# Layer 0 of a four-layer graph network: s products of two blocks issued together, the fifth slot group summed for four blocks, slot groups 172 columns apart

## The chip, the cores and the metric

One core of a Trainium2 chip runs the whole kernel in one launch. The metric is device time in microseconds (us). Five engines work side by side, each through its own queue in order: TensorE (PE, with its weight loads listed apart as PEld), VectorE (DVE), ScalarE (ACT), GpSimd (POOL) and SyncE (SP, which issues most DMAs). They wait for one another through semaphores.

## The reference, cut to what matters

A feature matrix x of 2708 rows by 128 columns goes through four layers with a sparse adjacency matrix adj of 2708 by 2708 (about 2.3% of its entries are not zero). Only layer 0 is touched by the change:

```python
s = node_feats @ msg_w[:, :D].T
d = node_feats @ msg_w[:, D:].T
messages = jax.nn.gelu(s[:, None, :] + d[None, :, :] + msg_b, approximate=False)
aggregated = jnp.einsum('ijd,ij->id', messages, adj)
combined = jnp.concatenate([node_feats, aggregated], axis=-1)
new_feats = combined @ upd_w.T + upd_b
h = jax.nn.gelu(new_feats, approximate=False) + node_feats
```

So for every edge (i, j) a gelu of s[i] + d[j] is needed, weighted by adj[i, j] and summed over j into row i. Layers 1 to 3 (gated attention, a hyperbolic layer, two propagation steps) follow.

## The kernel before

**Tiles and blocks.** Layer 0 takes the rows in 22 row tiles (LT) of 125 rows (LR), each as five groups (NC) of 25 rows (RG). The columns j are cut into 22 blocks (NB) of 124 (JB). In a block, each row has five slots (CAP); a slot holds one of the row's edges in the block. 25 rows times five slots fill 125 of 128 partitions, so a block's five groups of rows give five slot groups, each a set of columns of one PSUM tile `sl`: 128 columns for s + d and 25 columns for the edge weights (DA = 153). Edges beyond the five slots of a block go a second way: the largest 16 per row are searched out on DVE (`largest`, `where`), their d rows are fetched by indirect DMAs on POOL (`fetch`), and they are added by `far_gelu` (ACT) and `far_sum` (DVE).

**One block**, loop at L1021. `pick` (L944) multiplies one-hot selectors S (124 by 128, fp16, made on DVE by `slot`) with dA, the table of d and of the adjacency weights, in a high and a low fp16 part: ten products of 153 columns, one pair per slot group, into `sl`. Then two s products add s to the 128 columns of each group: `same` (50 rows, one-hot) times `s3`; s3 keeps groups 0 to 2 on partitions 0 to 49 and groups 3 and 4 on partitions 64 to 113, so one product uses the upper and one the lower half of the rows of the PE array. ACT takes a gelu of the block's message columns (L1028) into g; `weigh` (L1014) lets DVE multiply the 25 weight columns of each slot with `own`, which gives W. `add_up` (L957) sums over slots: per slot group, W (128 by 32) times g (128 by 128), fp32, into one PSUM bank `acc`. Its output is 32 partitions, so four groups use four column strips of the array side by side. It is called for a pair of blocks; groups 0 to 3 of both go to column 0 of acc, the fifth groups of both to column 1, on partitions 0 to 31 and 32 to 63.

**PSUM.** Three `sl` tiles of two banks each are used in turn (L1025), one bank is shared by `rank`, `rank_row` and `turn` (p_misc), one holds acc.

**Order.** Within `tc.manual_schedule()` each engine runs what is issued, in the order of the Python code. Everything around the block loop is a list of steps with a block number to be issued at (`Rows.when`, L748): loads of adjacency blocks (SP), masks and ranks (`find`, `rank`, `rank_row`: DVE, PE, ACT), selectors (`slot`), spilled edges (`past`, `largest_of`, `where`), for the following row tiles. In each pass of the loop the order is: steps due earlier, pick, gelu, weigh of the block before, steps due at this block; `late` collects blocks whose slot sums are outstanding, and LAG = 3 sends the sums of the oldest two after the steps of every even block. A row tile's sums end in `agg` (L971), which `turn` (L930) brings into transposed form, with `spread` and `fold` adding the 32-row strips.

Lines that the text names: L820 `rank`'s product, L821 its copy on ACT, L828 and L833 the high and low part of the adjacency weights (ACT, DVE), L840 selectors, L861 `rank_row`'s products, L872 `past`, L879 the block maxima, L910 the search, L914 the indirect fetch, L920 and L928 gelu and sums of the far edges, L950 picks, L955 s products, L966 slot sums, L1015 W, L1028 gelu.

Of the kernel before, what the change touches and what calls it, by code (L numbers as in the profile page):

```python
# [14 lines left out]
F32 = mybir.dt.float32  # L15
# [3 lines left out]
ALU = mybir.AluOpType  # L19
# [3 lines left out]
P = 128  # L23
# [149 lines left out]
def gnn_stack(ctx: ExitStack, tc: tile.TileContext, t, out: bass.AP):  # L173
# [378 lines left out]
    with ExitStack() as l0:  # L552
# [10 lines left out]
        with ExitStack() as msg:  # L563
# [4 lines left out]
            sq_tab = dram.tile([2, NT * P, D], FP16, name="sq_tab")  # L568


            DA = D + RG
            dA = [mp.tile([JB, NB, NC, DA], FP16, name=f"dA{q}") for q in range(2)]


# [53 lines left out]
            ep = msg.enter_context(tc.tile_pool(name="slots", bufs=5))  # L628
# [24 lines left out]
            class Piece:  # L653
# [7 lines left out]
                def products(self):  # L661
                    b0, b1, a0, a1 = self.b0, self.b1, self.a0, self.a1
                    psd, pss = (sl_all[(2 * self.n + k) % 3][:, 0, :].rearrange("p (b d) -> p b d", d=D)
                                for k in range(2))
                    d = self.d = ep.tile([P, 6, D], F32, name="g")[:JB, :b1 - b0, :]
                    room = gp.tile([P, 8, D], F32, name="far")
                    s = self.s = room[:, :a1 - a0, :]
                    parts = room[:, 4:, :].rearrange("p i d -> p (i d)").bitcast(FP16)
                    self.parts = parts.rearrange("p (q i d) -> p q i d", q=2, d=D)[:, :, :a1 - a0, :]
                    if N < b1 * JB:  # L670
                        nc.vector.memset(d, 0.0)
                    if N < a1 * P:
                        nc.vector.memset(s, 0.0)
                    for b in range(b0, b1):
                        r = min(JB, N - b * JB)
                        nc.tensor.matmul(psd[:r, b - b0, :], xT[:, b * JB:b * JB + r], msg_d, start=True, stop=True)
                    for i in range(a0, a1):
                        nc.tensor.matmul(pss[:rows[i], i - a0, :], xT[:, i * P:i * P + rows[i]], msg_s,
                                         start=True, stop=True)
                    full = min(b1, NFB) - b0  # L680
                    nc.scalar.copy(d[:, :full, :], psd[:JB, :full, :])
                    if full < b1 - b0:
                        r = N - NFB * JB
                        nc.scalar.copy(d[:r, full, :], psd[:r, full, :])
                    self.hi, self.lo = (v[:, b0:b1, :, :D] for v in dA)
                    nc.scalar.activation(self.hi[:, :, 0, :], d, AF.Copy, scale=D_SCALE)
                    self.spread(self.hi)
                    for a, b, r in groups():
                        if a0 <= a < a1:
# [12 lines left out]

                def update(self):
                    ps = p_out.tile([P, PB, D], F32, name="acc")
                    u = ep.tile([P, 6, D], F32, name="g")[:, :self.a1 - self.a0, :]
# [32 lines left out]
            class Rows:  # L738
# [191 lines left out]
                def turn(self):  # L930
# [3 lines left out]
                    nc.tensor.matmul(ps[:, :32 * NC], self.extra, spread.rearrange("p c i -> p (c i)"),  # L934
                                     start=True, stop=False)
                    nc.tensor.matmul(ps[:, :P], a[:, 0, :], ident, start=False, stop=False)
                    nc.tensor.matmul(ps[:, P:32 * NC], a[:HALF, 1, :], fold, start=False, stop=True)

                def close(self):
                    nc.scalar.copy(aggT[:, self.r0:self.r0 + LR].rearrange("p (c i) -> p c i", c=NC),  # L940
                                   self.ps_t[:, :32 * NC].rearrange("p (c i) -> p c i", c=NC)[:, :, :RG])


                def pick(self, b, sl):  # L944

                    h, n = divmod(b, HB)
                    group = [sl[:, c // 3, c % 3 * DA:(c % 3 + 1) * DA] for c in range(NC)]
                    for c in range(NC):
                        for q in range(2):
                            nc.tensor.matmul(group[c], self.S[h][:, n, c, :], dA[q][:, b, c, :],  # L950
                                             start=c % 3 == 0 and q == 0, stop=False)
                    for k, (a, e) in enumerate(spans(0, NC, 3)):
                        p = slice(k * HALF, k * HALF + 2 * RG)
                        out = sl[:, k, :(e - a) * DA].rearrange("p (c e) -> p c e", c=e - a)[:, :, :D]
                        nc.tensor.matmul(out, same[p], self.s3[p, :e - a, :], start=False, stop=True)  # L955

                def add_up(self, pair):  # L957


                    if pair[0][0] == 0:  # L960
                        self.acc = p_out.tile([P, PB, D], F32, name="acc")[:, :2, :]
                    jobs = [(b, g, W, c, c * 32, 0) for b, g, _, W in pair for c in range(4)]
                    jobs += [(b, g, W, 4, b % 2 * 32, 1) for b, g, _, W in pair]
                    for b, g, W, c, q, k in jobs:
                        ends = b == NB - 1 and q >= HALF or b >= NB - 2 and k == 1
                        nc.tensor.matmul(self.acc[q:q + 32, k, :], W[:, c, :], g[:, c, :],  # L966
                                         start=b == 0 and k == 0, stop=ends)
                    if pair[-1][0] == NB - 1:
                        self.agg = up.tile([P, 2, D], F32, name="agg")
                        for k, m in ((0, P), (1, HALF)):  # L970
                            nc.scalar.activation(self.agg[:m, k, :], self.acc[:m, k, :], AF.Copy,  # L971
                                                 accum_out=tot[:m, self.t, k:k + 1])

            class Update:

# [8 lines left out]
                    nc.sync.dma_start(out=self.new, in_=u_tab.rearrange("(n p) d -> p n d", p=P))  # L984

                def open(self):
                    room = Values.within(ep.tile([P, 6, D], F32, name="g").rearrange("p a d -> p (a d)"))
                    V = Values.within(ep.tile([P, 6, D], F32, name="g").rearrange("p a d -> p (a d)"))
# [20 lines left out]
            assert NC == 5 and NB % 2 == 0  # L1009
            R = [Rows(i) for i in range(LT)]  # L1010
            steps = sorted(((g, n, step) for n, (g, step) in enumerate(x for v in [preparation(), *(v.when() for v in R), U.when()] for x in v)),
                           key=lambda x: x[:2])
            with tc.manual_schedule():
                def weigh(b, g, sl, W):  # L1014
                    nc.vector.tensor_tensor(  # L1015
                        W[:, :, :RG].rearrange("p (k c) i -> p k c i", k=2), columns_of(sl, D, DA),
                        own[:, None, None, :].to_broadcast([P, 2, 3, RG]), op=ALU.mult)


                late = []  # L1020
                for block in range(LT * NB):  # L1021
                    i, b = divmod(block, NB)
                    while steps and steps[0][0] < block:
                        steps.pop(0)[2]()
                    sl, W = sl_all[block % len(sl_all)], W_all[block % len(W_all)]  # L1025
                    R[i].pick(b, sl)
# [919 lines left out]
```

## Time and profile before

| what | value |
|---|---|
| median of three runs | 1902.93 us (1902.68 to 1903.74) |
| the profiled execution | 1905.26 us, of it the span 1903.5 us |
| mean granted TensorE clock | 0.918 |
| PE busy over the span | 1626.2 us (85%) |
| DVE busy over the span | 1436.1 us (75%) |
| ACT / POOL busy over the span | 1052.1 us (55%) / 630.8 us (33%) |
| first and last pick of layer 0 | 55.5 us and 879.7 us |
| picks L950: count, busy | 4840, 408.2 us |
| slot sums L966: records, busy | 4840, 205.5 us (each product is two records) |
| s products L955: count, busy | 968, 161.9 us |
| gelu L1028: count, mean | 484, 813 ns |
| W L1015: count, mean | 484, 300 ns |

Busy times of PE overlap, since matmuls are pipelined and their ends are modelled; starts are exact. A mean over the whole span mixes layers with different limits, so the stretch from 55 to 880 us is what has to be read for this change. A line's "idle before" is the time for which its engine had nothing running just before it, with the release that ended it.

### The profile page before, as it was taken

The numbers are of one execution on the slowest core, as the hardware profiler recorded it, in microseconds if no ns is written. First come the engines' busy times: TensorE is split into PE (matmuls) and PEld (weight loads), VectorE is DVE, ScalarE is ACT, GpSimd is POOL, SyncE is SP. The second block draws the span as 40 slices with busy tenths as digits, with TensorE's granted clock in tenths as the row PEclk, the third lists the DMA queues.
The fourth block names the chain that finished last, engine by engine and source line by source line (L and its number), as shares of the span: only waits on it lengthen the run. The fifth ranks groups of instructions, "written<-read, shape, count | busy, mean of one in ns | idle before, by whom it ended". The sixth has DMA issues, their size and how long they took to land.

```text
span 1903.5 us, 36624 instructions
## 1 busy us (share of the span) xinstructions
PE 1626.2 (85%) x14033; PEld 955.4 (50%) x14033; DVE 1436.1 (75%) x3607; ACT 1052.1 (55%) x1538; POOL 630.8 (33%) x426
## 2 busy tenths in 40 slices
PE   5899999999999999986599997577888897199995
PEld 5666666666666666655344443322223343044542
DVE  6899999999999999986678885838886783860104
ACT  3667667666766766654444444458886771430003
POOL 5667766776776677565100000000000000000000
PEclk8899999999999999998699998658998798599997
DMA  8666665666666576533134430032334463354431
GB/s 214 153 130 143 133 144 119 148 122 141 143 131 142 122 149 124 117 69 88 63 123 150 152 112 1 1 106 76 142 137 140 141 199 146 137 204 146 146 121 31
DMA packets 234896, 238.30 MB, mean 125 GB/s; under 512 B 28844, under 2 KB 219630, under 8 KB 228122
## 3 DMA queue, kind: packets, MB, share of 16 engines
q1 hardware_dynamic: 183670, 212.18, 36.1%
q0 software_dynamic: 51040, 23.68, 10.7%
q8 instruction: 112, 1.84, 0.4%
q14 instruction: 74, 0.61, 0.1%
HBM read 220.65 MB, written 15.15 MB: 124 GB/s over the span
## 4 chain that ended last, share of the span: by engine, by line
PE 43%; DVE 28%; POOL 8%; issue 7%; ACT 7%; DMA 5%; DVEq 0%; SPq 0%; ACTq 0%; POOLq 0%
PE acc L1843 10%; POOL far L914 8%; PE lg L1231 5%; PE acc L1238 5%; PE accV L1571 5%; DVE ix L910 5%; PE ps L1499 4%; DMA far<-d_tab,ix 3%; DVE W L1015 3%; PE sl L950 3%; DVE extra L928 2%; DVE o L872 2%; DVE S L840 2%; PE accO L1575 2%; DVE dA L833 1%
## 5 line engine op out<-in xcount | busy, mean ns | idle before, releaser
L914 POOL DMA_INDIRECT far<-d_tab,ix x352 | 563.0, 1600 | 257.5 <-DVE W L1015 110.6
L1028 ACT ACTIVATE g<-sl 128x768 f32<-128x768 f32 x484 | 393.3, 813 | 257.0 <-PE sl L955 201.0
L950 PE MATMUL sl<-dA,S 124*128 124x153 f16 x4840 | 408.2, 231 | 10.1 <-DVE W L1015 7.7
L950 PEld LDWEIGHTS <-S 124*128 124x128 f16 x4840 | 330.4, 98 | 79.7 <-issue 67.9
L966 PE MATMUL acc<-g,W 128*32 128x128 f32 x4840 | 205.5, 277 | 0.5 <-issue 0.5
L966 PEld LDWEIGHTS acc<-g,W 128*32 128x32 f32 x4840 | 140.6, 109 | 58.8 <-issue 55.5
L955 PE MATMUL sl<-s,same 50*128 50x384 f16 x968 | 161.9, 308 | 0.0
L1015 DVE TENSOR_TENSOR W<-sl,own 128x150 f32<-128x150 f32 x484 | 143.4, 300 | 14.6 <-ACT g L1028 13.4
L1232 ACT ACTIVATE w<-lg,row_L_gnn_gate_bias 128x512 f32<-128x512 f32 (+1 forms) x132 | 83.5, 636 | 108.2 <-PE lg L1231 106.9
L1486 POOL TENSOR_TENSOR arena<-arena,off 128x128 f32<-128x128 f32 (+1 forms) x22 | 21.6, 982 | 351.1 <-DMA arena<-in_adjT 321.3
L840 DVE TENSOR_SCALAR S<-rk 124x1000 f16<-124x1000 bf16 (+1 forms) x330 | 133.4, 430 | 0.0
L910 DVE FIND_INDEX8 ix<-v,o 128x8 uint32<-128x2728 f32 x44 | 131.7, 2993 | 0.0
L1571 PE MATMUL accV<-arena,X 128*128 128x512 f32 (+4 forms) x264 | 124.7, 592 | 6.5 <-DVE arena L1537 6.5
L1231 PE MATMUL lg<-qT,mT 128*128 128x512 f32 (+2 forms) x264 | 121.1, 547 | 3.6 <-ACT w L1232 3.1
L1238 PE MATMUL acc<-w,both 128*128 128x512 f32 (+2 forms) x264 | 121.2, 547 | 0.0
L928 DVE SCALAR_TENSOR_TENSOR extra<-far,v,extra 128x128 f32<-128x128 f32 x330 | 114.9, 348 | 6.3
L449 DVE TENSOR_TENSOR g<-ps,row_L_gnn_b 128x512 f32<-128x512 f32 (+2 forms) x14 | 7.9, 574 | 148.1 <-PE ps L447 148.0
L1499 PE MATMUL ps<-XT 128*128 128x512 f32 (+8 forms) x150 | 90.4, 691 | 32.2 <-ACT arena L1505 26.5
L872 DVE SCALAR_TENSOR_TENSOR o<-ps,ar 128x496 f32<-128x496 f32 x132 | 82.4, 624 | 37.0 <-issue 19.7
L1843 PE MATMUL acc<-at,x 128*128 128x512 f32 (+2 forms) x156 | 66.2, 574 | 48.4 <-ACT x L379 48.4
L1233 DVE TENSOR_TENSOR w<-w,at 128x512 f32<-128x512 f32 (+1 forms) x132 | 82.5, 625 | 27.1 <-ACT w L1232 27.1
L879 DVE MAX8 cand<-o 128x8 f32<-128x248 f32 x242 | 90.4, 411 | 0.0
(357 smaller groups left out, 2507.2 us busy)
## 6 DMA issues: line engine op xcount, KB each, us to landing
at<-in_adjT SPq DMA_DIRECT2D x42, 1354.0 KB
ar<-in_adj SPq DMA_DIRECT2D x105, 248.0 KB
far<-s_tab SPq DMA_DIRECT2D x44, 512.0 KB
at<-in_adjT SPq DMA_DIRECT2D x42, 448.0 KB
arena<-in_adjT SPq DMA_DIRECT2D x21, 704.0 KB
arena<-in_adjT SPq DMA_DIRECT2D x21, 650.0 KB
held<-in_adjT SPq DMA_DIRECT2D x7, 1354.0 KB
f_tab<-arena SPq DMA_DIRECT2D x10, 704.0 KB
```

The costliest lines, as they stand in the source:

```text
L840: nc.vector.tensor_scalar(self.S[h][:, :n, :, k * RG:(k + 1) * RG], self.rk[h][:, :n, :LR].rearrange("p b (c i) -> p b c i", c=NC), EDGE + ...
L910: nc.vector.max_index(ix, self.v[:, n * 8:n * 8 + 8], self.o.rearrange("p b j -> p (b j)"))
L914: nc.gpsimd.indirect_dma_start(out=self.far[n][:, k, :], out_offset=None, in_=d_tab[:, :], in_offset=bass.IndirectOffsetOnAxis(ap=self.ix[ ...
L950: nc.tensor.matmul(group[c], self.S[h][:, n, c, :], dA[q][:, b, c, :], start=c % 3 == 0 and q == 0, stop=False)
L966: nc.tensor.matmul(self.acc[q:q + 32, k, :], W[:, c, :], g[:, c, :], start=b == 0 and k == 0, stop=ends)
L1015: nc.vector.tensor_tensor(W[:, :, :RG].rearrange("p (k c) i -> p k c i", k=2), columns_of(sl, D, DA), own[:, None, None, :].to_broadcast([ ...
L1028: nc.scalar.activation(g.rearrange("p (k c) d -> p k c d", k=2), columns_of(sl, 0, D), AF.Gelu, scale=1.0 / D_SCALE)
L1231: nc.tensor.matmul(lg, mT[:, j * P:j * P + r], qT[:, a:b], start=True, stop=True)
L1238: nc.tensor.matmul(acc[k], mrow[:rows[j], j, :], ws[j][:rows[j], a:b], start=j == 0, stop=j == NT - 1)
L1499: nc.tensor.matmul(ps, XT[:, self.js], XT[:, c], start=True, stop=False)
L1571: nc.tensor.matmul(Pair.acc[0][:, a:b], X[:self.r, self.j, :], self.w_[:, a:b], start=first, stop=last)
L1843: nc.tensor.matmul(acc[k], src[:rows[j], j, :], at[:rows[j], a:b], start=j == order[0], stop=j == order[-1])
```

## The change

1. `begin` (new) issues the s products of two blocks, ahead of their picks, at every even block: for block b and b + 1, in their two `sl` tiles. They now start the accumulation (start=True) and cover all 153 columns of a group, since `s3` is kept with 25 zero columns per group (two tiles, zeroed once on POOL). The picks all add to that.
2. In the pair, the order becomes: s products of both blocks, picks of the first, its steps, picks of the second, its steps, and the slot sums of the pair before (LAG = 2, sent at odd blocks).
3. `add_up` keeps the fifth slot groups until four blocks have them (or the row tile ends, which it does with two), and puts them on four strips of 32 partitions. The second column of acc and of agg has 128 rows in place of 64, and `fold` adds four strips.
4. Slot groups start 172 columns apart over the two banks of an `sl` tile (0, 172, 344, 516, 688), so gelu and `weigh` handle five groups with one step, 640 and 125 elements per partition, where they handled six places, 768 and 150.
5. W has six tiles in place of five, and so has the pool of g.

```diff
-            DA = D + RG
+            DA, PITCH = D + RG, 172
...
-            fold = mp.tile([HALF, 32], F32, name="fold")
-            nc.vector.tensor_add(fold, ident[:HALF, :32], ident[:HALF, 32:HALF])
+            fold = mp.tile([P, 32], F32, name="fold")
+            nc.vector.tensor_add(fold, ident[:, :32], ident[:, 32:HALF])
+            for k in range(HALF, P, 32):
+                nc.vector.tensor_add(fold, fold, ident[:, k:k + 32])
...
-            W_all = [mp.tile([P, 6, 32], F32, name=f"W{n}") for n in range(5)]
+            W_all = [mp.tile([P, NC, 32], F32, name=f"W{n}") for n in range(6)]
+            s3_all = [mp.tile([P, 3, DA], FP16, name=f"s3{n}") for n in range(2)]
+            for v in s3_all:
+                nc.gpsimd.memset(v, 0.0)
...
-                return sl[:, :, :3 * DA].rearrange("p k (c e) -> p k c e", c=3)[:, :, :, a:b]
+                return sl.rearrange("p k n -> p (k n)")[:, :NC * PITCH].rearrange("p (c e) -> p c e", c=NC)[:, :, a:b]
...
-                    self.s3 = up.tile([P, 3, D], FP16, name="s3")
+                    self.s3 = s3_all[self.t % 2]
...
-                            nc.sync.dma_start(out=self.s3[p:p + RG, :e - a, :], in_=src[:, a:e, :])
+                            nc.sync.dma_start(out=self.s3[p:p + RG, :e - a, :D], in_=src[:, a:e, :])
...
-                    nc.tensor.matmul(ps[:, P:32 * NC], a[:HALF, 1, :], fold, start=False, stop=True)
+                    nc.tensor.matmul(ps[:, P:32 * NC], a[:, 1, :], fold, start=False, stop=True)
...
+                def begin(self, sl):
+
+                    for k, (a, e) in enumerate(spans(0, NC, 3)):
+                        p = slice(k * HALF, k * HALF + 2 * RG)
+                        nc.tensor.matmul(columns_of(sl, 0, DA)[:, a:e, :], same[p], self.s3[p, :e - a, :], start=True, stop=False)
+
                 def pick(self, b, sl):
 
                     h, n = divmod(b, HB)
-                    group = [sl[:, c // 3, c % 3 * DA:(c % 3 + 1) * DA] for c in range(NC)]
                     for c in range(NC):
                         for q in range(2):
-                            nc.tensor.matmul(group[c], self.S[h][:, n, c, :], dA[q][:, b, c, :],
-                                             start=c % 3 == 0 and q == 0, stop=False)
-                    for k, (a, e) in enumerate(spans(0, NC, 3)):
-                        p = slice(k * HALF, k * HALF + 2 * RG)
-                        out = sl[:, k, :(e - a) * DA].rearrange("p (c e) -> p c e", c=e - a)[:, :, :D]
-                        nc.tensor.matmul(out, same[p], self.s3[p, :e - a, :], start=False, stop=True)
+                            nc.tensor.matmul(columns_of(sl, 0, DA)[:, c, :], self.S[h][:, n, c, :], dA[q][:, b, c, :], start=False,
+                                             stop=q == 1 and c in (2, NC - 1))
...
-                    jobs += [(b, g, W, 4, b % 2 * 32, 1) for b, g, _, W in pair]
+                    self.fifth += [(b, g, W, 4, b % 4 * 32, 1) for b, g, _, W in pair]
+                    if len(self.fifth) == 4 or b1 == NB - 1:
+                        jobs += self.fifth
+                        self.fifth = []
...
-            LAG = 3
+            LAG = 2
...
+                    if b % 2 == 0:
+                        for k in range(2):
+                            R[i].begin(sl_all[(block + k) % len(sl_all)])
                     R[i].pick(b, sl)
-                    g = ep.tile([P, 6, D], F32, name="g")
-                    nc.scalar.activation(g.rearrange("p (k c) d -> p k c d", k=2), columns_of(sl, 0, D), AF.Gelu,
+                    g = ep.tile([P, NC, D], F32, name="g")
+                    nc.scalar.activation(g, columns_of(sl, 0, D), AF.Gelu,
                                          scale=1.0 / D_SCALE)
```

More of the change, by code (lines that the diff above doesn't have):

```diff
@@ L627, in gnn_stack @@
             up = msg.enter_context(tc.tile_pool(name="sums", bufs=2))
-            ep = msg.enter_context(tc.tile_pool(name="slots", bufs=5))
+            ep = msg.enter_context(tc.tile_pool(name="slots", bufs=6))
             p_misc = msg.enter_context(tc.tile_pool(name="ps_misc", bufs=1, space=PSUM))
@@ L664, in products @@
                                 for k in range(2))
-                    d = self.d = ep.tile([P, 6, D], F32, name="g")[:JB, :b1 - b0, :]
+                    d = self.d = ep.tile([P, NC, D], F32, name="g")[:JB, :b1 - b0, :]
                     room = gp.tile([P, 8, D], F32, name="far")
@@ L704, in update @@
                     ps = p_out.tile([P, PB, D], F32, name="acc")
-                    u = ep.tile([P, 6, D], F32, name="g")[:, :self.a1 - self.a0, :]
+                    u = ep.tile([P, NC, D], F32, name="g")[:, :self.a1 - self.a0, :]
                     if N < self.a1 * P:
@@ L941, in close @@
                                    self.ps_t[:, :32 * NC].rearrange("p (c i) -> p c i", c=NC)[:, :, :RG])
+                def begin(self, sl):
+                    for k, (a, e) in enumerate(spans(0, NC, 3)):
+                        p = slice(k * HALF, k * HALF + 2 * RG)
+                        nc.tensor.matmul(columns_of(sl, 0, DA)[:, a:e, :], same[p], self.s3[p, :e - a, :], start=True, stop=False)
                 def pick(self, b, sl):
                     h, n = divmod(b, HB)
-                    group = [sl[:, c // 3, c % 3 * DA:(c % 3 + 1) * DA] for c in range(NC)]
                     for c in range(NC):
                         for q in range(2):
-                            nc.tensor.matmul(group[c], self.S[h][:, n, c, :], dA[q][:, b, c, :],
-                                             start=c % 3 == 0 and q == 0, stop=False)
-                    for k, (a, e) in enumerate(spans(0, NC, 3)):
-                        p = slice(k * HALF, k * HALF + 2 * RG)
-                        out = sl[:, k, :(e - a) * DA].rearrange("p (c e) -> p c e", c=e - a)[:, :, :D]
-                        nc.tensor.matmul(out, same[p], self.s3[p, :e - a, :], start=False, stop=True)
+                            nc.tensor.matmul(columns_of(sl, 0, DA)[:, c, :], self.S[h][:, n, c, :], dA[q][:, b, c, :], start=False,
+                                             stop=q == 1 and c in (2, NC - 1))
                 def add_up(self, pair):
-                    if pair[0][0] == 0:
+                    b1 = pair[-1][0]
+                    if b1 == 1:
                         self.acc = p_out.tile([P, PB, D], F32, name="acc")[:, :2, :]
+                        self.fifth = []
                     jobs = [(b, g, W, c, c * 32, 0) for b, g, _, W in pair for c in range(4)]
-                    jobs += [(b, g, W, 4, b % 2 * 32, 1) for b, g, _, W in pair]
+                    self.fifth += [(b, g, W, 4, b % 4 * 32, 1) for b, g, _, W in pair]
+                    if len(self.fifth) == 4 or b1 == NB - 1:
+                        jobs += self.fifth
+                        self.fifth = []
                     for b, g, W, c, q, k in jobs:
@@ L967, in add_up @@
                                          start=b == 0 and k == 0, stop=ends)
-                    if pair[-1][0] == NB - 1:
+                    if b1 == NB - 1:
                         self.agg = up.tile([P, 2, D], F32, name="agg")
-                        for k, m in ((0, P), (1, HALF)):
-                            nc.scalar.activation(self.agg[:m, k, :], self.acc[:m, k, :], AF.Copy,
-                                                 accum_out=tot[:m, self.t, k:k + 1])
+                        for k in range(2):
+                            nc.scalar.activation(self.agg[:, k, :], self.acc[:, k, :], AF.Copy,
+                                                 accum_out=tot[:, self.t, k:k + 1])
             class Update:
@@ L986, in open @@
                 def open(self):
-                    room = Values.within(ep.tile([P, 6, D], F32, name="g").rearrange("p a d -> p (a d)"))
-                    V = Values.within(ep.tile([P, 6, D], F32, name="g").rearrange("p a d -> p (a d)"))
+                    room = Values.within(ep.tile([P, NC, D], F32, name="g").rearrange("p a d -> p (a d)"))
+                    V = Values.within(ep.tile([P, NC, D], F32, name="g").rearrange("p a d -> p (a d)"))
                     self.st = room.part([P, NT, 6])
@@ L1005, in rows @@
                     nc.gpsimd.tensor_tensor(x[:r, a:b, :], x[:r, a:b, :], over_tiles(ln_b, b - a, r), op=ALU.add)
-            LAG = 3
+            LAG = 2
             U = Update()
-            assert NC == 5 and NB % 2 == 0
+            assert NC == 5 and NB % 4 == 2
             R = [Rows(i) for i in range(LT)]
@@ L1015, in weigh @@
                     nc.vector.tensor_tensor(
-                        W[:, :, :RG].rearrange("p (k c) i -> p k c i", k=2), columns_of(sl, D, DA),
-                        own[:, None, None, :].to_broadcast([P, 2, 3, RG]), op=ALU.mult)
+                        W[:, :, :RG], columns_of(sl, D, DA), own[:, None, :].to_broadcast([P, NC, RG]),
+                        op=ALU.mult)
                 late = []
@@ L1025, in gnn_stack @@
                     sl, W = sl_all[block % len(sl_all)], W_all[block % len(W_all)]
+                    if b % 2 == 0:
+                        for k in range(2):
+                            R[i].begin(sl_all[(block + k) % len(sl_all)])
                     R[i].pick(b, sl)
-                    g = ep.tile([P, 6, D], F32, name="g")
-                    nc.scalar.activation(g.rearrange("p (k c) d -> p k c d", k=2), columns_of(sl, 0, D), AF.Gelu,
+                    g = ep.tile([P, NC, D], F32, name="g")
+                    nc.scalar.activation(g, columns_of(sl, 0, D), AF.Gelu,
                                          scale=1.0 / D_SCALE)
```

## The prediction

> **What bounds the kernel now.** Only layer 0 is edited, so I first read the busy time by stretch: layer 0's steady part, its last row tile but one, its last, and everything behind it (columns: length; busy time and instructions of PE, PEld, DVE, ACT, POOL; clock; DMA).
>
> ```profile
> 60.00:800.00 740.00, 705.80 (x10288) 507.02 (x10286) 696.67 (x1984) 504.75 (x752) 513.47 (x321) 1.00 0.65 134
> 800.00:845.00 45.00, 37.66 (x538) 26.58 (x536) 39.41 (x110) 26.65 (x39) 20.02 (x13) 1.00 0.39 86
> 845.00:885.00 40.00, 36.51 (x549) 27.25 (x547) 23.46 (x69) 22.28 (x35) 30.59 (x20) 1.00 0.48 87
> 885.00:1905.00 1020.00, 812.12 (x2468) 364.55 (x2466) 632.35 (x1357) 478.26 (x679) 36.62 (x35) 0.86 0.33 117
> ```
>
> Two engines are full at once: PE 95% and DVE 94% of the steady part, at full clock; ACT (68%) is not. The starts of the first pick in each row tile lie 37.03 us apart (20 of the 22 tiles are near that; tile 20 takes 43.7). So a PE saving is worth only what DVE can follow. The timeline of one pair of blocks gives PE's prices (start, length, engine, line; ends are modelled, so I use start to next start):
>
> ```profile
> 402.83 0.85 PE L966 MATMUL acc<-g,W 128*32 128x128 f32 x20
> ...
> 403.61 0.65 PEld L950 LDWEIGHTS <-S 124*128 124x128 f16 x10 [0.20 <-issue]
> 403.61 0.84 PE L950 MATMUL sl<-dA,S 124*128 124x153 f16 x10
> ...
> 404.39 0.33 PE L955 MATMUL sl<-s,same 50*128 50x384 f16 x2
> ...
> 404.66 0.39 PE L861 MATMUL ps<-tri,mask 124*128 124x125 bf16 x4
> ...
> 404.89 0.83 PE L950 MATMUL sl<-dA,S 124*128 124x153 f16 x10
> ...
> 405.65 0.33 PE L955 MATMUL sl<-s,same 50*128 50x384 f16 x2
> ```
>
> There is no hole: slot sums 0.78, picks 0.78, s products 0.27, four rank products 0.23, picks 0.76, s products 0.26. Within them, by the start times of single records: picks come every 67 ns, but the s product starts 162 ns after the last pick, so a change of array shape costs about 95 ns; the two s products start 3 ns apart (they use different row halves and run side by side) and the next group starts 0.26 later; the 20 sum records form six waves 109 ns apart, four wide, the last two waves (the fifth slot group) two wide, and 0.205 passes after the last.
>
> Then DVE, where a run of long instructions shows what it does to the order, and where it idles (groups of 100 to 740 us):
>
> ```profile
> 431.90 0.30 DVE L1015 TENSOR_TENSOR W<-sl,own 128x150 f32<-128x150 f32 x1
> 432.11 0.08 DVE L910 MATCH_VALUE_LOAD ix<-v,o 128x8 f32 x1
> 432.18 2.99 DVE L910 FIND_INDEX8 ix<-v,o 128x8 uint32<-128x2728 f32 x1
> 435.09 0.52 DVE L1015 TENSOR_TENSOR W<-sl,own 128x150 f32<-128x150 f32 x2
> 435.52 0.08 DVE L910 MATCH_VALUE_LOAD ix<-v,o 128x8 f32 x1
> 435.59 2.99 DVE L910 FIND_INDEX8 ix<-v,o 128x8 uint32<-128x2728 f32 x1
> 438.50 0.29 DVE L1015 TENSOR_TENSOR W<-sl,own 128x150 f32<-128x150 f32 x1
> ```
> ```profile
> L872 DVE SCALAR_TENSOR_TENSOR o<-ps,ar 128x496 f32<-128x496 f32 x104 | 65.1, 626 | 25.8 <-issue 19.2 <-PE sl L955 4.8 <-PE ps L861 1.6
> ```
>
> W products (L1015) stand in order behind 3 us searches. DVE's only real idle time is before L872, about 1.6 us once a tile (block 15), where it waits for rank products that PE has not reached. Start to start, DVE's own work is 34.9 us per tile. PE's holes are also about 1.6 us per tile, most before one L820 at block 18, which waits for an ACT copy. So PE sets the pace in about half of a tile and DVE in the other, with three slot buffers between them.
>
> **The change, part by part.**
> *s products of two blocks first.* Per pair before: pick to s 0.162 and s to next 0.263, twice: 0.85. After: four s products, of which the second two follow on the same row halves. Their 459 columns (with the zero columns) stream in 191 ns (384 take 0.263 less a drain of about 0.10: 160 ns; times 459/384), so the group takes 0.19 + 0.29 = 0.48; picks to picks 0.067; picks to sums 0.162: 0.71. Saved 0.13 per pair. *A rule against it:* the Trainium skill (TensorE: Matmul & The Clock Gate, "The mechanism") says that LDWEIGHTS overlaps in-flight matmuls only when the row group differs. The second two reload the same row halves, so by the rule their load (92 ns) is exposed and the saving is 0.04. The fence above has ten loads of 124 rows within 0.65 us beside ten matmuls of the same rows; I take the row, 0.13.
> *Fifth group for four blocks.* Waves: two per pair before; after, two at six of a tile's eleven pairs (the last with two blocks). Five pairs save 2 x 109 ns: 1.09 per tile.
> *PE in sum:* 11 x 0.13 + 1.09 = 2.5 per tile, and fold over 128 rows drops a change of shape in the turn (0.1). PE's work falls from 37.03 - 1.6 = 35.4 to 32.85.
> *Pitch 172.* W has 125 elements in place of 150. The two forms of L872 (496 elements 0.67, 248 elements 0.42) give 1 ns per element: 25 ns x 22 = 0.55 off DVE's 34.93: 34.38. Gelu has 640 in place of 768: by L1028 (813 ns) against the 1024 of L920 (1049) 0.92 ns per element, by L821's two forms 0.70; so about 0.71 us. That takes 2.2 us per tile from an engine with room; it counts only as latency.
> *Setup:* three fold additions and two POOL memsets lie beside the opening loads: nothing; at most 1 us. load_s issues the same four DMAs of 256-byte rows on SP: nothing.
> *The new wait.* With three slot buffers, block 2p+1 reuses that of block 2p-2. Its s product now stands ahead of pick(2p), so pick(2p), all behind it on PE, and their gelus wait for W of block 2p-2; before, PE had two blocks more to do before that wait. Call the start of that s product B, the end of W(2p) T. From B to T: s 0.29, nine pick steps 0.60, last pick to gelu 0.33, gelu 0.71, W with its start 0.30: 2.25 at least. So per round T = max(T' + D, B + 2.25), and the next B = max(B + C, T + 0.05), where T' is the previous T and D is DVE's work in between. D for the eleven rounds, from DVE's starts: 2.53 3.36 4.21 2.82 3.36 3.34 1.88 2.40 3.58 3.03 3.87 (4.21 holds a search). C, PE's own: 1.97 for s products, picks and changes of shape, 0.58 or 0.80 for sums, 0.12 to 0.33 for rank products, 0.9 for the turn: 3.01 2.79 3.00 2.78 3.01 2.79 3.00 3.68 3.01 2.68 3.11. Going round until it repeats: rounds 1 to 5 and 10 are DVE's without a hole; in rounds 6 to 8 PE is late and DVE idles about 0.35, 0.5 and 0.2. The tile takes 35.5. To that come 0.25 for L872 of block 15, which still stands behind the turn, and DVE's small start gaps (0.35 in all, most on the path): 35.9 to 36.0.
> The L820 hole at block 18 closes: sums and s products, 1.2 us, now stand between the two L820. What is late next is DVE.
>
> *Sum.* 37.03 - 35.9 = 1.1 for 20 tiles: 22. Tile 20, where DVE is loaded with extra memsets and PE already waits for W: 0.5. The last tile has little DVE work, so PE's 2.5 counts: 2 to 2.5. Together 25. Against the span of 1903.5 (1905.26 with what lies around it; the median 1902.93 is 0.1% below) this is the median less 25: **1878**.
>
> **The rivals.**
> *DVE never starved.* If buffers and timing let DVE run without a hole: 34.38 + 0.35 = 34.7, 2.3 per tile: 46 + 3 = 49, so 1854. For it: the chain of waits over one tile (392.5 to 429.5 us) has 52% on DVE's lines and 25% on PE's; against it: rounds 6 to 8, where DVE's work (1.88, 2.40) is below PE's 3.0 and 3.7.
> *The s group costs more* (the skill's exposed load, or slow strided writes): 0.09 per pair is 1 us of C per tile, of which the four or five rounds set by PE show about 0.4: 8 us back, 1886.
> *Slower: the early s product closes the ring.* One mechanism: the loop B to T is longer than 2.25, because gelu of the even block stands behind other ACT work. Today gelu of blocks 4, 10 and 18 starts 0.65 to 0.87 later after its picks than the usual 0.31, behind L828 (1.07) and L821 (0.57). If every loop took 3.0, the same rounds give 37.1, with the same additions 37.6: 20 x 0.6 - 2 = 10 us slower, 1913. The turning point is a loop of about 2.85. Against it: those three blocks lie in rounds with D of 4.21, 3.34 and 3.03, which cover 2.25 + 0.75.
>
> **How the numbers follow.** Forecast (1866 to 1892) 0.55; DVE never starved 0.18; dearer s group 0.14; slower 0.13. Range 1853 to 1902: it takes in the first three and leaves out most of the slower case. A difference under 0.2% (3.8 us) can't be told from none: faster than that 0.84, within it 0.04, slower 0.12.
>
> **What would show it.** s groups of four with the next group 0.48 after the first; picks of two blocks 67 ns apart; sums of 12 and 8 products in turn, 0.80 and 0.58; gelu 0.71; tiles of 36 us; PE idle of 2 to 3 us per tile before the s products, released by W, above all around the searches; L872's hole shrinking to about 0.3; DVE at 96%. Wrong if that PE idle exceeds 4 us per tile, if DVE's idle stays at 2 us, or if even gelus start over 1 us after their picks.

## The result and the profile after

| | before | after |
|---|---|---|
| median of four runs | 1902.81 us (1901.2 to 1903.74) | 1880.58 us (1879.03 to 1881.93) |
| the profiled execution, its span | 1905.26 us, 1903.5 us | 1879.03 us, 1877.3 us |
| mean granted TensorE clock | 0.918 | 0.920 |
| first and last pick | 55.5 and 879.7 us | 54.0 and 855.5 us |
| period of a row tile (median of tiles 2 to 19) | 37.03 us | 36.04 us |

The ratio of the runs is 0.9884 (95% interval 0.9867 to 0.9901): 22 us faster. In the two profiled executions layer 0's last pick comes 24.2 us earlier. By the starts of the first picks of the row tiles, 18.4 us of that come from tiles 2 to 19; the start and tile 0 give 3.1, tile 1 takes 0.2 back, tile 20 takes 1.1 more (43.7 to 44.8 us), and from the first pick of the last tile to its last one it is 4.0 shorter (35.3 to 31.2). The start is no reading: over all the traces of this text the first pick lies between 53.0 and 56.0 us, whatever the edit.

The busy time by stretch of the changed kernel, over the same stages as before (steady part, last tile but one, last tile, the other layers):

```profile
60.00:780.00 720.00, 668.66 (x10316) 480.84 (x10315) 694.62 (x1988) 456.64 (x751) 532.73 (x321) 1.00 0.65 138
780.00:822.00 42.00, 34.13 (x477) 24.05 (x475) 34.73 (x97) 22.18 (x37) 19.38 (x12) 0.92 0.43 88
822.00:860.00 38.00, 35.64 (x568) 26.18 (x566) 24.04 (x71) 20.97 (x37) 30.59 (x20) 1.00 0.48 90
860.00:1877.00 1017.00, 811.43 (x2468) 364.27 (x2467) 632.05 (x1357) 478.40 (x679) 38.62 (x36) 0.86 0.33 117
```

In the steady part PE has gone from 95% to 93%, though tiles follow faster, and DVE from 94% to 96%: the two are no longer level. The same queue of PE, as a timeline of two pairs (lines of PE, and the W for which it waits):

```profile
407.91 0.56 PE L953 MATMUL sl<-s,same 50*128 50x459 f16 x4
...
408.40 1.51 PE L960 MATMUL sl<-dA,S 124*128 124x153 f16 x20
...
409.75 0.38 PE L825 MATMUL ps<-mask,tri 124*128 124x512 bf16 x1
...
410.06 0.86 PE L977 MATMUL acc<-g,W 128*32 128x128 f32 x24
...
410.86 0.56 PE L953 MATMUL sl<-s,same 50*128 50x459 f16 x4
...
411.35 0.84 PE L960 MATMUL sl<-dA,S 124*128 124x153 f16 x10
...
413.00 0.65 PE L977 MATMUL acc<-g,W 128*32 128x128 f32 x16
...
413.58 0.37 PE L953 MATMUL sl<-s,same 50*128 50x459 f16 x2
413.78 0.28 DVE L1026 TENSOR_TENSOR W<-sl,own 128x125 f32<-128x125 f32 x1
...
414.12 0.35 PE L953 MATMUL sl<-s,same 50*128 50x459 f16 x2 [0.17 <-DVE W L1026]
```

Start to start the forecast's prices stand here one by one: four s products 0.49 (407.91 to 408.40; 0.48 forecast), 20 picks in a row 1.35 (67 ns each), sums of twelve products (24 records) 0.80 and of eight (16 records) 0.58. The group at 413.58 breaks after two products: the third needs the slot buffer that W of an earlier block still reads. That is the forecast's new wait.

The groups from 100 to 740 us (busy and mean, then idle time before them and its releasers):

```profile
L977 PE MATMUL acc<-g,W 128*32 128x128 f32 x3900 | 155.9, 278 | 9.8 <-DVE W L1026 8.0
...
L953 PE MATMUL sl<-s,same 50*128 50x459 f16 (+1 forms) x780 | 120.5, 331 | 14.0 <-DVE W L1026 12.2
...
L1026 DVE TENSOR_TENSOR W<-sl,own 128x125 f32<-128x125 f32 x391 | 106.2, 275 | 8.8 <-ACT g L1042 8.8
...
L877 DVE SCALAR_TENSOR_TENSOR o<-ps,ar 128x496 f32<-128x496 f32 x106 | 66.0, 623 | 3.7 <-PE ps L866 3.7
...
L866 PE MATMUL ps<-tri,mask 124*128 124x125 bf16 x394 | 39.4, 219 | 12.7 <-DVE count L879 12.7
```

DVE's hole before `past` (L872 before, L877 now) fell from 25.8 us to 3.7; the largest part of what is left of DVE's idle time, 8.8 us, stands before W. PE is idle ahead of slot sums, s products and rank products for 36.5 us in these 640 by the modelled ends, and DVE ends 32.9 of them. Counted from start to start, with the shortest course of each group as its work, all of PE's holes are 4.0 us per tile; before they were 1.6, most of them a wait for ACT ahead of L820. The busy time from the first pick of tile 2 to that of tile 20, 18 tiles, before and after (columns as above, DVE is the third busy time):

```profile
133.00:800.80 667.80, 638.10 (x9326) 458.80 (x9325) 630.43 (x1802) 457.09 (x684) 459.91 (x288) 1.00 0.64 134
```
```profile
130.10:779.50 649.40, 603.73 (x9326) 434.18 (x9326) 629.64 (x1804) 413.84 (x684) 480.54 (x288) 1.00 0.65 138
```

DVE is busy for 35.02 us a tile before and 34.98 after, and idle for 2.08 and 1.10. **The whole gain of 1.0 us per tile is idle time of DVE that closed; its work did not get less.** The timeline around a search shows PE waiting for DVE's queue:

```profile
420.40 3.00 DVE L915 FIND_INDEX8 ix<-v,o 128x8 uint32<-128x2728 f32 x1
...
423.02 0.43 PE L977 MATMUL acc<-g,W 128*32 128x128 f32 x8
423.31 0.47 DVE L1026 TENSOR_TENSOR W<-sl,own 128x125 f32<-128x125 f32 x2
...
423.63 0.43 PE L977 MATMUL acc<-g,W 128*32 128x128 f32 x8 [0.19 <-DVE W L1026]
```

The slot sums stop in their middle until the W behind the search is there.

### The profile page after: what moved, and what is told of

It reads as the page before. It is cut to its first block, busy times and chain, and to the rows that moved or that the text cites. A ratio compares the mean times of both kernels' runs of the same rounds, so it can differ in the third digit from the quotient of the medians.

```text
span 1877.3 us, 36661 instructions
## 1 busy us (share of the span) xinstructions
PE 1581.1 (84%) x14033; PEld 921.2 (49%) x14033; DVE 1432.4 (76%) x3609; ACT 999.4 (53%) x1538; POOL 653.2 (35%) x429
## 3 DMA queue, kind: packets, MB, share of 16 engines
q1 hardware_dynamic: 183670, 212.18, 36.2%
## 4 chain that ended last, share of the span: by engine, by line
PE 38%; DVE 7%; ACT 6%; issue 1%; DMA 0%; ACTq 0%; DVEq 0%
PE acc L1857 11%; PE lg L1245 5%; PE acc L1252 5%; PE accV L1585 5%; PE ps L1513 4%; PE accO L1589 2%; PE ps L1568 1%; ACT arena L1519 1%; DVE arena L1547 1%; PE ps L1514 1%; ACT x L379 1%; DVE arena L1571 1%; PE ps L447 1%; PE ps_w L1213 1%; ACT arena L1540 0%
## 5 line engine op out<-in xcount | busy, mean ns | idle before, releaser
L919 POOL DMA_INDIRECT far<-d_tab,ix x352 | 583.1, 1657 | 217.3 <-issue 97.0
L1042 ACT ACTIVATE g<-sl 128x640 f32<-128x640 f32 x484 | 335.4, 703 | 297.3 <-PE sl L960 272.5
L960 PE MATMUL sl<-dA,S 124*128 124x153 f16 x4840 | 380.9, 233 | 0.0
L960 PEld LDWEIGHTS <-S 124*128 124x128 f16 x4840 | 326.0, 98 | 72.0 <-issue 69.8
L977 PE MATMUL acc<-g,W 128*32 128x128 f32 x4840 | 194.5, 280 | 15.5 <-DVE W L1026 13.5
L953 PE MATMUL sl<-s,same 50*128 50x459 f16 x968 | 150.5, 333 | 17.8 <-DVE W L1026 15.5
L977 PEld LDWEIGHTS acc<-g,W 128*32 128x32 f32 x4840 | 117.4, 109 | 70.4 <-DVE W L1026 27.5
L1026 DVE TENSOR_TENSOR W<-sl,own 128x125 f32<-128x125 f32 x484 | 131.2, 275 | 21.6 <-ACT g L1042 21.6
L845 DVE TENSOR_SCALAR S<-rk 124x1000 f16<-124x1000 bf16 (+1 forms) x330 | 141.4, 455 | 0.0
L933 DVE SCALAR_TENSOR_TENSOR extra<-far,v,extra 128x128 f32<-128x128 f32 x330 | 114.6, 347 | 6.8 <-ACT far L925 0.5
L877 DVE SCALAR_TENSOR_TENSOR o<-ps,ar 128x496 f32<-128x496 f32 x132 | 82.0, 621 | 12.2 <-DMA ar<-in_adj 6.8
```

What stands on the lines that cost most here:

```text
L845: nc.vector.tensor_scalar(self.S[h][:, :n, :, k * RG:(k + 1) * RG], self.rk[h][:, :n, :LR].rearrange("p b (c i) -> p b c i", c=NC), EDGE + ...
L919: nc.gpsimd.indirect_dma_start(out=self.far[n][:, k, :], out_offset=None, in_=d_tab[:, :], in_offset=bass.IndirectOffsetOnAxis(ap=self.ix[ ...
L953: nc.tensor.matmul(columns_of(sl, 0, DA)[:, a:e, :], same[p], self.s3[p, :e - a, :], start=True, stop=False)
L960: nc.tensor.matmul(columns_of(sl, 0, DA)[:, c, :], self.S[h][:, n, c, :], dA[q][:, b, c, :], start=False, stop=q == 1 and c in (2, NC - 1))
L1042: nc.scalar.activation(g, columns_of(sl, 0, D), AF.Gelu, scale=1.0 / D_SCALE)
```

## The experiments

My theory on seeing the result: DVE has become the pace, and most of the saving on PE is idle time of PE now. The rival: PE still sets the end through its waits, and each of the parts gives its share. Every experiment is an edit of the changed kernel (e1 to e7, e11) or of the kernel before (e8 to e10, e12). Ratios are to the kernel before, with 95% intervals; "tile" is the median period of tiles 2 to 19.

**e1: the fifth slot group for two blocks again.**

```diff
-                    if len(self.fifth) == 4 or b1 == NB - 1:
+                    if True:
```

> The changed kernel, but the fifth slot groups are summed with every pair again. PE gets back 5 x 2 waves of 109 ns, 1.09 us per row tile, nothing else changes. Theory 1 (DVE paces a tile of 36.0 us, PE has about 3 us of holes): at most 0.2 us per tile, 1880 to 1885, and PE's waits for W shrink. Rival (PE's work still sets the time): 22 x 1.09 = 24 us more, about 1904.

Measured: 1880.16 us, ratio 0.9879 (0.9862 to 0.9895), tile 36.03. The steady part, from 100 to 740 us, of the changed kernel and of e1:

```profile
100.00:740.00 640.00, 595.14 (x9195) 428.06 (x9192) 619.34 (x1780) 408.24 (x672) 476.35 (x286) 1.00 0.65 139
```
```profile
100.00:740.00 640.00, 609.44 (x9199) 446.24 (x9197) 619.32 (x1778) 408.54 (x672) 477.14 (x286) 1.00 0.67 138
```

PE has 14 us more to do, DVE the same 97%, and the time is the same. The saving of the fifth groups, forecast at 1.09 us per tile, is worth nothing here by itself.

**e2: s products of each block by itself.**

```diff
-                    if b % 2 == 0:
-                        for k in range(2):
-                            R[i].begin(sl_all[(block + k) % len(sl_all)])
+                    R[i].begin(sl)
```

> The changed kernel, but the s products of a block stand right before its own picks. PE gets back 0.13 us per pair or more (a change of shape more per block), 1.4 to 2 us per tile, and the ring of slot buffers is as loose as before. Theory 1 (DVE paces): PE's holes take it up, 1876 to 1888; the loss through the tight ring is small. Rival A (PE paces): 30 to 40 us more, 1910 or above. Rival B (the early s products cost much through their wait for W): the time falls by 10 us or more, below 1870.

Measured: 1881.42 us, ratio 0.9881 (0.9864 to 0.9897), tile 35.97, PE busy 623 of 640 us. Nothing either. So each of the two savings on PE can go and the time stays.

**e5: both undone.** The edits of e1 and e2 together; what stays of the change is the order (s products ahead of the picks, sums after the odd block), the pitch of 172 columns with its shorter W and gelu, the fold over 128 rows, and the sixth buffers of W and g.

> The changed kernel with both savings of PE undone: fifth groups with every pair, s products block by block. Left are the pitch of 172 (W 25 ns and gelu 0.11 us shorter) and the sums after odd blocks. PE's work is back at 35.2 to 35.4 us per tile against DVE's 35.0. Theory 1 (each saving alone was worth nothing because either one brings PE under DVE; together they are the gain): PE and DVE are level again, tile 36.4 to 36.8, 1887 to 1897. Rival (the gain never came from PE's work but from the shorter W and gelu): 1884 or below, as with one undone.

Measured: 1886.27 us, ratio 0.9913 (0.9896 to 0.9929), tile 36.16. Steady part:

```profile
100.00:740.00 640.00, 633.51 (x9160) 448.19 (x9161) 610.70 (x1775) 411.05 (x670) 458.26 (x285) 1.00 0.68 138
```

PE is full again, its holes about 0.6 us per tile, yet only 6 us are lost, just under the range of the theory and above that of the rival. So 17 of the 22 us do not need the two savings at all.

**e3: W with its old 150 elements.** The weights' columns are read and multiplied 30 wide in place of 25, five of them zero.

```diff
-            own = mp.tile([P, RG], F32, name="own")
+            own = mp.tile([P, 30], F32, name="own")
+            nc.vector.memset(own, 0.0)
...
-W[:, :, :RG], columns_of(sl, D, DA), own[:, None, :].to_broadcast([P, NC, RG]),
+W[:, :, :30], columns_of(sl, D, D + 30), own[:, None, :].to_broadcast([P, NC, 30]),
```

> The changed kernel, but W's product handles 30 columns per group in place of 25, so 150 elements per partition as in the kernel before; the five more are zeros. DVE gets back 25 ns per block, 0.55 us per tile. Theory 1 (DVE paces): nearly all of it shows, 8 to 12 us, 1889 to 1892. Rival (PE or the waits of the ring pace): under 3 us.

Measured: 1885.56 us, ratio 0.9908 (0.9892 to 0.9925), tile 36.31: 5 us, half of what 0.55 us of DVE per tile for 20 tiles comes to, and in neither range. The masks' mean went down from 816 to 729 ns in this run, which gives part of it back; e6 is about that.

**e4: the masks on ACT.** `find` is the one long DVE step that ACT can take as it is: the sign of a non-negative number is its mask.

```diff
-                    nc.vector.tensor_scalar(self.mask[h][:, :n, :], self.at[h][:, :n, :], 0.0, None,
-                                            op0=ALU.not_equal)
+                    nc.scalar.activation(self.mask[h][:, :n, :], self.at[h][:, :n, :], AF.Sign)
```

> The changed kernel, but the three masks of a row tile are made on ACT (Sign) instead of DVE. DVE loses about 2.1 us per tile, ACT (64% busy) gains about 3. Theory 1 (DVE paces): the tile falls towards PE's 32.8, to 34.5 or so: 1845 to 1860. Rival (ring and PE pace): under 8 us, 1872 or more. If gelus stand too long behind masks on ACT, something between.

Measured: **1856.7 us**, ratio 0.9757 (0.974 to 0.9773), tile 34.76. Steady part, and two groups of the same stretch:

```profile
100.00:740.00 640.00, 610.82 (x9501) 437.15 (x9498) 601.04 (x1784) 464.95 (x751) 468.76 (x295) 1.00 0.70 144
```
```profile
L1025 DVE TENSOR_TENSOR W<-sl,own 128x125 f32<-128x125 f32 x404 | 109.6, 275 | 26.4 <-ACT g L1041 17.4 <-issue 7.2
...
L817 ACT ACTIVATE mask<-at 124x1024 bf16<-124x1024 f32 (+1 forms) x55 | 53.9, 980 | 0.0
```

The step is dearer on ACT (0.98 us in place of 0.73), and gelus come later for it: DVE's idle time before W went from 8.8 to 26.4 us. It is a gain of 24 us all the same, since DVE had the work and ACT had room. This shows what paces the changed kernel, and it is faster than both kernels.

**e7 and e11: the savings on PE, with DVE relieved.** e7 is e4 with both savings undone as in e5, e11 is e4 with the edit of e2.

> Masks on ACT, and both savings of PE undone. With DVE relieved by 2 us per tile, PE's 2.5 us per tile must show. Theory 1: PE paces at 35.3 and more, tile 36.0 to 36.6, 1880 to 1893, that is 25 to 35 us above masks on ACT alone (1856.7). Rival (ring and latencies pace there): below 1868.

> Masks on ACT, fifth groups for four blocks, s products block by block: the wait for W comes later in PE's order, PE has 1.4 us per tile more work. Theory 1 (with masks on ACT the tile of 34.8 is set by DVE and by the tight ring together, PE 32.8): the loose ring gives back about what PE loses, 1852 to 1862. Rival (PE's work sets it): 1872 or above.

Measured: e7 1874.79 us (ratio 0.9851, 0.9835 to 0.9868; tile 35.68, PE busy 636.5 of 640), e11 1859.81 us (0.9765, 0.9749 to 0.9782; tile 34.76, PE busy 635). The two savings that cost 6 us when undone in the changed kernel cost 18 once DVE has less to do: what a saving on PE is worth depends on which engine paces. The time of e7 falls between the two ranges of e7, nearer the theory's. One of the two, the fifth group, is enough for e4's time: e11's interval covers it.

**e6: no far rows fetched.** The indirect fetch on POOL issues nothing, so the d rows of far edges are left out of the result; all of DVE's instructions stay.

```diff
-                    for k in range(8):
-                        nc.gpsimd.indirect_dma_start(
...
-                            compute_op=ALU.add)
+                    pass
```

> The changed kernel without the indirect fetches on POOL (the d rows of the far edges are left out; their gelu and sums still run). Theory: masks and selectors (2-byte outputs, L817 and L845) take longer while POOL's fetch is under way; without it every mask of 1024 takes 0.675 us and every selector of 1000 0.41, DVE's work falls by about 0.6 to 1.0 us per tile, and as DVE paces the time falls by 10 to 20 us, 1860 to 1870. Rival (their length has another cause): means stay at 0.81 and 0.48, time within 5 us of 1880.

Measured: 1863.87 us, ratio 0.9797 (0.9781 to 0.9813), tile 35.39. Selectors and full masks by shape, in the kernel before, in the changed one and in e6 (100 to 740 us):

```profile
L840 DVE TENSOR_SCALAR S<-rk 124x1000 f16<-124x1000 bf16 x170 | 70.0, 440 | 0.0
...
L840 DVE TENSOR_SCALAR S<-rk 124x750 f16<-124x750 bf16 x85 | 31.4, 369 | 0.0
...
L812 DVE TENSOR_SCALAR mask<-at 124x1024 bf16<-124x1024 f32 x34 | 24.9, 731 | 0.0
```
```profile
L845 DVE TENSOR_SCALAR S<-rk 124x1000 f16<-124x1000 bf16 x180 | 80.9, 479 | 0.0
...
L845 DVE TENSOR_SCALAR S<-rk 124x750 f16<-124x750 bf16 x90 | 34.7, 386 | 0.0
...
L817 DVE TENSOR_SCALAR mask<-at 124x1024 bf16<-124x1024 f32 x35 | 28.6, 816 | 0.0
```
```profile
L845 DVE TENSOR_SCALAR S<-rk 124x1000 f16<-124x1000 bf16 x180 | 71.9, 428 | 0.0
...
L845 DVE TENSOR_SCALAR S<-rk 124x750 f16<-124x750 bf16 x90 | 32.5, 361 | 0.0
...
L817 DVE TENSOR_SCALAR mask<-at 124x1024 bf16<-124x1024 f32 x36 | 24.3, 676 | 0.0
```

Without the fetch a full mask takes 676 ns; in the kernel before 731, in the changed kernel 816. Per tile (ten, five and two of them) the change made these three groups longer by 0.39 + 0.09 + 0.17 = 0.65 us. The one short mask of a tile went the other way, by 0.14 us:

```profile
L812 DVE TENSOR_SCALAR mask<-at 124x768 bf16<-124x768 f32 x17 | 11.7, 690 | 0.0
```
```profile
L817 DVE TENSOR_SCALAR mask<-at 124x768 bf16<-124x768 f32 x18 | 9.9, 552 | 0.0
```

The balance of 0.5 us is as much as W's 0.55 saved. That is where the shorter W went. The overlap in time goes with it: a fetch lies over 54% of the full masks' time before and over 97% after, and over 99% of the short mask's time before and 76% after.

**e9 and e12: the order by itself, in the kernel before.** e9 only sets LAG to 2, so that the sums of a pair follow the odd block.

```diff
-            LAG = 3
+            LAG = 2
```

e12 does that, keeps s3 with zero columns, and puts the s products ahead of the picks in each block:

```diff
+                    for k, (a, e) in enumerate(spans(0, NC, 3)):
+                        p = slice(k * HALF, k * HALF + 2 * RG)
+                        out = sl[:, k, :(e - a) * DA].rearrange("p (c e) -> p c e", c=e - a)
+                        nc.tensor.matmul(out, same[p], self.s3[p, :e - a, :], start=True, stop=False)
                     for c in range(NC):
                         for q in range(2):
...
-                                             start=c % 3 == 0 and q == 0, stop=False)
-                    for k, (a, e) in enumerate(spans(0, NC, 3)):
...
-                        nc.tensor.matmul(out, same[p], self.s3[p, :e - a, :], start=False, stop=True)
+                                             start=False, stop=q == 1 and c in (2, NC - 1))
```

> The kernel before with one figure changed: LAG = 2, so that the sums of a pair come after odd blocks. No engine has less work. Theory 1 (the change's gain came for the larger part from closing PE's hole of 1.1 us per tile before the second L820, because sums now stand between the two): the hole shrinks to 0.3 us, tile 36.2 to 36.5, 1885 to 1893. Rival (ACT closed it, through gelus that are 0.11 us shorter): the hole stays above 0.8, 1898 to 1906.

> The kernel before with its order alone changed: in every block the s products stand ahead of the picks, the slot sums of a block follow the picks of the next one (a lag of 2 in place of 3), each block by itself; the s product of three groups is padded with 25 columns of zeros so that it covers what the picks add to. W keeps its 150 columns, gelu its 768, the fifth slot group is summed for two blocks. Theory (most of what is left with both PE savings undone comes from the order: no further change of shape is added, and the hole of 1.1 us before the ninth block's rank product is closed): a tile of 36.3 to 36.5 us, 1887 to 1892 us. Rival (the order is worth no more than the shorter lag alone, and the rest comes from the shorter W and gelu): as the lag alone, 1895 to 1899 us.

Measured: e9 1897.61 us (ratio 0.9967, 0.9956 to 0.9977; tile 36.79), e12 1896.14 us (0.9956, 0.9939 to 0.9972; tile 36.63). The groups of `rank`'s product in the kernel before and in e9:

```profile
L820 PE MATMUL ps<-mask,tri 124*128 124x512 bf16 (+1 forms) x103 | 38.1, 369 | 19.1 <-ACT rk L821 17.2 <-DVE ar L854 0.7 <-ACT aggT L940 0.4
```
```profile
L820 PE MATMUL ps<-mask,tri 124*128 124x512 bf16 x104 | 38.5, 370 | 6.2 <-ACT rk L821 3.0 <-DVE mask L812 0.9 <-DVE ar L854 0.4
```

The wait for ACT ahead of L820 closed as forecast (17.2 to 3.0 us, 0.8 per tile), but PE's own work grew by about 0.6 us per tile: sums now stand right behind rank products, one more change of array shape each (a slot sum starts 148 ns after the last product of `rank_row`, where a pick starts 55 ns after it in the kernel before). So the 0.8 us per tile bring 0.24, and e9 lies between its two ranges, next to the rival's. Having the s products ahead adds hardly more (e12, in the rival's 1895 to 1899; of both kernels the sums of a pair, not of a single block, as the expectation has it, come after the odd block). The order alone is worth 6 to 8 of the 17 us. The other 9 or so are left to what e5 has and e12 has not: W of 125 elements (worth 5 by e3, in the changed kernel), gelu of 640, and one change of shape less in the turn. The last two were not tried alone. The sixth buffers of W and g are no candidate: from 100 to 740 us no step of the kernel before, of e9 or of e12 waits for a slot sum to free one.

**e8: the masks on ACT, in the kernel before.** The edit of e4.

> The kernel before with its masks on ACT, nothing else. DVE falls from 34.9 to 32.8 us per tile, PE stays at 35.4. Theory 1 (PE set about half of the tile's pace before): the tile falls from 37.0 towards PE's work, 36.0 to 36.7: 1880 to 1897. Rival (DVE set it all): 24 us as in the changed kernel, below 1880. Rival (PE set it all): no gain, 1900 or above.

Measured: 1890.51 us, ratio 0.9933 (0.9916 to 0.995), tile 36.50. Half of e4's 24 us: there PE stands in the way, and the hole of 1.1 us at block 18 remained.

**e10: fewer fifth-group sums, in the kernel before.** The fifth slot groups of five of the eleven pairs are not summed, so a part of the aggregate is missing; PE saves what the change saves there.

```diff
-                    jobs += [(b, g, W, 4, b % 2 * 32, 1) for b, g, _, W in pair]
+                    if pair[-1][0] % 4 == 1 or pair[-1][0] == NB - 1:
+                        jobs += [(b, g, W, 4, b % 2 * 32, 1) for b, g, _, W in pair]
```

> The kernel before with the fifth sums of five of a tile's eleven pairs left out (part of the aggregate is missing): PE loses 1.09 us per tile, as by the change's third item, and nothing else moves. Theory 1 (before, PE with its hole set the pace): a third to three quarters of it shows, 1886 to 1897, while in the changed kernel it was worth nothing. Rival (DVE set the pace before, too): under 4 us, 1899 or above.

Measured: 1894.85 us, ratio 0.9956 (0.994 to 0.9973), tile 36.62. The same sums are worth 0.41 per tile and 8 to 10 us here, and by e1 nothing once the rest of the change is in. The worth of a part depends on which parts are there already; a sum of parts measured one at a time isn't the whole.

## Why the prediction was right, and where its terms were off

1. **The sum and the sign held, the sum in part by luck.** 1.1 us per tile were forecast and 1.0 came; 25 us in all, and the profiled executions differ by 26.2 in their spans, the medians by 22.2. That PE's saving of 2.5 us per tile would not be paid out in full, since DVE has nearly as much to do, was right: e1, e2 and e4 show it. But the forecast gave that saving too large a part. Its own rounds, with the 2.5 us put back evenly, give a tile of 36.2 in place of 35.5; e5 puts both savings back and the tile is 36.16 in place of 36.04 (e5 loosens the ring of slot buffers as well). Of the 22 us, 17 stay without that saving.

2. **PE's prices held, its sum was too high.** The group of four, the picks without a gap and the two sizes of sums are in the timeline above, near the forecast's numbers. The rule of the Trainium skill (TensorE: Matmul & The Clock Gate, "The mechanism") that was weighed there would have had the second two loads exposed and a group 0.09 longer; the trace has 0.49, so the row decided rightly, and the rival built on that rule is out. PE's work per tile is 36.04 less 4.0 of holes, 32.0, where I had 32.85. A part of it is the turn: its first product starts 0.07 after a pick, where it started 0.64 after an s product before (some 0.3 of that a wait), and the forecast had 0.1 for it. The rest I did not trace.

3. **The wait came where it was put.** "PE idle of 2 to 3 us per tile before the s products, released by W": 1.5 before the third s product and 0.95 in the slot sums, 2.4 in all. A further 0.95 before the rank products of block 21 (L866, waiting for `count` on DVE to free its PSUM bank) and 0.56 before `rank` at block 9 were not in the forecast. Together with 0.1 at block 18 that is 4.0. The bar of 4, past which I would have called the step wrong, was set on the part released by W.

4. **DVE's work was mis-sized, and so was its idle time, in opposite ways.** "25 ns x 22 = 0.55 off DVE's 34.93: 34.38": W did become 25 ns shorter (300 to 275), yet DVE's work stayed at 35.0, since selectors and masks took 0.5 longer in all beside the fetch (e6). On the other side "in rounds 6 to 8 PE is late and DVE idles about 0.35, 0.5 and 0.2", plus 0.25 and 0.35, made some 1.6 us of idle time; it is 1.10: 0.4 before W in place of the rounds' 1.05, 0.2 before `past`, the rest in small gaps. The faster PE explains only a part of that, for the rounds with 35.0 of DVE and 32.0 of PE still leave about 0.9; the rest stays open. The two errors cancel, 34.38 + 1.6 and 34.98 + 1.10 are 36.0 and 36.1, and that is luck.

5. **Latencies held.** Gelu takes 0.703 us (0.71 forecast). It starts 0.04 after the end of its picks, as the trace models that end, where it was 0.31 before: the s products and a change of shape no longer lie between. Only at block 7 it starts 0.9 later. The loop from the third s product to the end of W takes 2.19 where W does not stand in DVE's queue, 2.25 in the forecast. The slower rival, which needed 2.85 through late gelus of even blocks, never came near: these start 1.17 to 1.23 after the third s product.

6. **The hole at block 18 closed** (1.14 to 0.1), for the reason given; but e9 shows that the same reordering without the rest would have cost most of it again in changes of shape.

7. **The ends of layer 0.** The last tile gave 4.0 in place of 2 to 2.5. Tile 20 lost 1.1 where 0.5 of gain was forecast: there PE waits for a mask and the spilled edges for a DMA of `ar`, and why both come later than before stays open. The fetches have a part in it, since in e6 the tile takes 39.2 in place of 44.8. Up to the end of tile 19 the change brings 21.3 of the forecast's 22, and 1.5 of that lie ahead of the first pick, which is no reading.

8. **The fast rival** (DVE never starved, 1854) was right about the engine that paces and wrong about its work: with 34.98 + 0.35 in place of 34.38 + 0.35 it gives 35.3 per tile, and DVE still idles 0.4 before W, waiting for gelus, and 0.2 before `past`.

## What to carry to other kernels

When two engines are level, price a saving on one by what the other can follow, then look for work that can leave the engine that will pace: the masks moved to ACT (e4, 1856.7 us) were worth as much as the whole change. Test the parts of a change one at a time and also all together: here either saving on PE alone could go for nothing, both cost 6 us, and with DVE relieved 18. A step made shorter on a busy engine need not shorten the engine's work, if others then run more often beside something that slows them; compare the engine's work per tile, not the one row.

## What the runs showed of the hardware that was not expected

- Masks and selectors on DVE (one tensor in, a 2-byte output) become longer beside POOL's indirect fetches: the 124x1024 mask takes 0.675 us where no fetch overlaps and 0.82 in the mean (up to 0.96) where one covers it all; a 124x1000 selector 0.42 where a fetch covers a part of it and 0.49 where it covers it all. Steps with two tensor inputs do not, whatever their output: in the changed kernel and without the fetches (e6) the fp16 L838 of 1000 columns takes 1.188 and 1.194, the fp32 L933 0.347 and 0.347, W 0.275 and 0.277. The Trainium skill (SBUF — State Buffer, "SBUF: two separate sides") says that a DVE operation in a mode that uses two ports, or with two inputs from SBUF where the GpSimd operation reads SBUF too, and a GpSimd operation hold a shared pair of ports exclusively, one blocking the other. Its first case fits which steps grow, if masks and selectors run in such a mode, which no trace here shows; L838 and L933 have two inputs from SBUF and show nothing of the second. The growth, 0.07 to 0.15 in the mean, is far less than a fetch's 1.66. e6 took the transfers away with the fetches, so it does not separate the ports from the traffic.
- Two s products that reload row halves still in use follow the two before them after 0.14 us at the shortest, but the group of four takes 0.49 at the shortest all the same.
- A change of array shape between kinds of products can cost nearly as much as a reordering brings: e9 closed 0.8 us of waiting per tile and paid 0.6 of it back.
